# The last two pairs of a combined four-layer convolution: PSUM tiles, copies and output thirds rearranged

## The chip, the cores and the metric

The kernel runs on one core of a Trainium2 chip. The metric is the device time of one execution in microseconds (us), and the time of a kernel is the median of its runs. Engines are named as in the profile: PE is TensorE's matmul, PEld its weight load, DVE is VectorE, ACT is ScalarE, POOL is GpSimd, SP is SyncE, whose queue issues the transfers.

## What is computed

A batch of 128 samples, each with 64 channels of 1024 positions, goes through four convolutions of 3 taps. They are of the types same, upsample, same and downsample, with a blur of four taps beside each change of the rate. The weights of each layer are scaled by a style of the sample and normalised (demodulated), so each sample has its own weights. The input is added to the result.

```python
s = style @ mw.T + mb
weight = SCALE * w * s[:, None, :, None]
demod = lax.rsqrt(jnp.sum(weight * weight, axis=(2, 3)) + EPS)
weight = weight * demod[:, :, None, None]
...
for i, typ in enumerate(TYPES):
    out = _layer(out, style, weights[i], biases[i], mod_w[i], mod_b[i], typ)
return out
...
x = x + _L0_cond_ref(x, cond_512, L0_cond_weights, L0_cond_biases, L0_cond_mod_w, L0_cond_mod_b)
```

All data are float32.

## The kernel before, in words

**One convolution for four.** Between the ends of the signal, four linear layers are one convolution of 9 taps with a 64 x 64 matrix per tap and sample. The kernel builds these weights on TensorE for four samples at a time (a quad, index q, 32 of them): stage1, stage2 and stage3 multiply the weights of the layers into each other, and each stage's PSUM result is scaled and copied to SBUF by ACT (line 330). The result is `Wf`. combine (lines 452 to 463) makes three sums of it, h1, h2 and h3 in tile `H`, on DVE. The few positions near the ends are computed apart, spread over the rounds, and do not touch the change.

**Pairs of samples.** The convolution itself runs over pairs of samples (index p, 64 of them, two per quad). The positions of a sample lie in three planes (position modulo 3), and in two halves of 170 per plane. A fast scheme gives the three output planes with five products instead of nine:

- pre1 and pre2 (lines 480 to 526) form the five combinations of the input planes, tile `T`, on DVE and POOL;
- product (line 528) is one of the five products: 12 matmuls in each of two banks, one bank for each sample of the pair (a float32 matmul has two records in the profile, so 48 records are two products and 24 are one);
- convA12 computes products 1 and 2 and convA3 product 3 into the tile `psA`; convA3 also has ACT copy the first product, negated, to SBUF (`m1`, line 567);
- seed (seed1 and seed2, lines 572 to 599, all through line 573) combines the three on DVE: it makes `u` and `v`, writes the third output plane `y1` to SBUF, and writes a start value of the first two planes into a PSUM tile (`Y` in the profile). seed_last does the same in another order, the PSUM part first;
- convB adds products 0 and 4 onto the start values in PSUM;
- output (line 622) scales and shifts the planes into the tile `o`: planes 0 and 1 from PSUM in one instruction of 340 columns, the third from `y1` in one of 170 columns. On ACT that is line 630, on DVE line 632;
- store (line 634) issues the transfer of one sample to memory from SP's queue. It waits for the output of that sample, and later stores wait behind it.

[...] Fresh banks therefore get matmuls of zeros first (zeros_to_y, line 164, matmuls at line 170).

**PSUM.** There are eight banks of 512 columns. The pool `ps_conv` has two tiles of two banks each (`psA`, in turn for even and odd pairs), `ps_y` has the one tile `Y` of two banks, and `ps_w` has two tiles of one bank each, which the weight stages use. The helper unit gives two banks of a pool:

```python
if pool is ps_w:
    return [pool.tile([P, 512], F32, tag=f"u{r}", name=f"{name}_{r}") for r in range(2)]
t = pool.tile([P, 2, 512], F32, tag="u", name=name)
return [t[:, r, :] for r in range(2)]
```

So two banks from `ps_w` are two tiles, and two banks from `ps_conv` are one tile. All pairs use `Y` except those in the dictionary Y2, which y_bank (line 161) looks up. When the weight stages have ended, the banks of `ps_w` are free: before, pairs 60 and 62 have these, and pair 63 takes a `ps_conv` tile (Y3). Pair 61 uses `Y`.

**The order.** The order of the program is the order on each engine's queue (manual_schedule), and the framework adds the waits between the engines. A round q of the loop at line 1061 runs convB and the outputs of pairs 2q and 2q+1, convA12 and convA3 of the pairs after them, and the weight stages of later quads. In the last three rounds:

- round 29 (p = 58) makes the last weights; the zeros go to the banks of pair 60 (lines 1130 to 1134), then seed(60), combine(31), convA12(61) and convA3(61);
- round 30 (p = 60, the branch q == NQ - 2) runs convB(60), the outputs of 60, convA12(62), seed(61), pre2(63), convA3(62), convA12(63), convB(61), output(61, 0) by ACT, seed(62), convA3(63), the zeros of 63, output(61, 1) by DVE and seed_last(63);
- round 31 (p = 62, q == NQ - 1) runs convB(62), its outputs by ACT and DVE, convB(63), and the outputs of 63 plane by plane: third, first, second, sample 0 by ACT and sample 1 by DVE each time. The first two planes are stored apart, so 63 has four stores, two of 170 columns and two of 340.

Of the kernel before, what the change touches and what calls it, by code (L numbers as in the profile page):

```python
# [49 lines left out]
AF = mybir.ActivationFunctionType  # L50
# [13 lines left out]
def kernel(  # L64
# [13 lines left out]
    NQ = B // 4  # L78
# [5 lines left out]
    nc_v, nc_a, nc_g = nc.vector, nc.scalar, nc.gpsimd  # L84
# [13 lines left out]
    ps_conv = ctx.enter_context(tc.tile_pool(name="ps_conv", bufs=2, space=PSUM))  # L98
# [48 lines left out]
    def unit(pool, name):  # L147
# [7 lines that stand above are left out]
    NB = 170  # L155
# [3 lines left out]
    Y2 = {}  # L159

    def y_bank(p, s):
        return Y2[p][s] if p in Y2 else Y[:, s]

    def zeros_to_y(sets, n, p=0):


        for i in range(sets):
            rows = HALF[i % 2]
            for cols in HALF:
                nc.tensor.matmul(  # L170
                    y_bank(p, i % 2)[cols, :n], Z[rows, :C], Z[rows, :n], start=True, stop=True
                )
# [51 lines left out]
    def var_inverse(bs, ls=slice(0, NL)):  # L224
        nc_v.reciprocal(dm[:, ls, bs], nw[:, ls, bs])
# [241 lines left out]
    HO = 3 * NB  # L467
    Ts = {}
    Gs = {}
    part = {}  # L470
# [53 lines left out]
    def pre2(p):  # L524
        pre2a(p)
        pre2b(p)

    def product(p, m, ps):

        W, H_ = Wq[p // 2]  # L530
        r0 = p % 2
        for g in range(3):
            for s, rows in enumerate(HALF):
                for h, cols in enumerate(HALF):
                    if m in (0, 4):
                        w = W[rows, r0, K * g + m // 2, :]
                    else:
                        w = H_[rows, m - 1, r0, g, :]
                    j = NB * h + g
                    nc.tensor.matmul(  # L540
                        ps[s][cols],
                        w,
                        Ts[p][rows, SLOT[m], j : j + NB],
                        start=(g == 0 and m not in (0, 4)),
                        stop=(g == 2),
                        skip_group_check=True,
                    )

    def m_tile(tag, p, shape=(2, NB)):
        return mpool.tile([P, *shape], F32, tag=tag, name=f"{tag}_{p}")  # L550

    def convA12(p):
        if p >= NP:
            return
        ps = ps_conv.tile([P, 2, 512], F32, tag="u", name=f"psA{p}")
        m = [ps[:, :, i * NB : (i + 1) * NB] for i in range(3)]
        product(p, 1, [m[0][:, s] for s in range(2)])
        product(p, 2, [m[1][:, s] for s in range(2)])
        part[p] = m

    def convA3(p):
        if p >= NP:
            return
        m = part[p]
        product(p, 3, [m[2][:, s] for s in range(2)])
        m1 = m_tile("m1", p)
        nc_a.activation(m1, m[0], AF.Copy, scale=-1.0)  # L567
        part[p] = (m1, *m[1:])

    y1s = {}  # L570

    def sum_of(out, x, f, y):
        nc_v.scalar_tensor_tensor(out, x, f, y, op0=ALU.mult, op1=ALU.add)  # L573
# [12 lines left out]
    def seed2(p):  # L586
        if p >= NP:
            return
        m3, u = part.pop(p)
        banks = [(slice(s, s + 1), y_bank(p, s)[:, None]) for s in range(2)]  # L590
        if p not in Y2:
            banks = [(slice(0, 2), Y)]
        for i, f in enumerate((1.0 / 6.0, 4.0 / 6.0)):
            for k, y in banks:
                sum_of(y[..., i * NB : (i + 1) * NB], m3[:, k], f, u[:, k])

    def seed(p):
        seed1(p)
        seed2(p)

    def seed_last(p):

        m1, m2, m3 = part.pop(p)
        u, v = m_tile("u", p), m_tile("v", p)
        y1s[p] = mpool.tile([P, 2, NB], F32, tag="y1", name=f"y1_{p}", bufs=3)
        sum_of(u, m2, -1.0 / 3.0, m1)
        part[p] = m3, u
        seed2(p)
        sum_of(v, m2, 1.0 / 3.0, m1)
        sum_of(y1s[p], m3, 2.0 / 6.0, v)  # L610
# [11 lines left out]
    def output(p, s, eng=nc_a, parts=((0, 2), (2, 3))):  # L622

        b = 2 * p + s
        d3, add = dm[:, 3, b : b + 1], oc[:, b : b + 1]
        for i, j in parts:
            dst = os[p][:, s, i * NB : j * NB]
            src = y1s[p][:, s] if i == 2 else y_bank(p, s)[:, i * NB : j * NB]
            if eng is nc_a:
                nc_a.activation(dst, src, AF.Identity, bias=add, scale=d3)  # L630
            else:
                eng.tensor_scalar(dst, src, d3, add, op0=ALU.mult, op1=ALU.add)

    def store(p, s, at=slice(0, 3 * NB)):
        nc.sync.dma_start(out[p, :, s, at], os[p][:, s, at])
# [100 lines left out]
    def zeros():  # L736
        for t in Ye:
            nc_g.memset(t[:, :, 0:1], 0.0)
            nc_g.memset(t[:, :, 7:8], 0.0)
        for t in Ue:  # L740
            nc_g.memset(t[:, :, 0:1], 0.0)
            nc_g.memset(t[:, :, 10:11], 0.0)
        for t in Ve:
            nc_g.memset(t[:, :, 0:2], 0.0)
            nc_g.memset(t[:, :, 10:12], 0.0)
        nc_g.memset(g1, 0.0)
# [142 lines left out]
    BOTH = nc_a, nc_v  # L889
# [171 lines left out]
    for q in range(NQ):  # L1061
        p = 2 * q
        c, s = q + 2, q + 3
        if q == 1:
            nc.sync.dma_start(Xe, x_ends)
        if q == 5:
            zeros()
        if c < NQ:
            stage2(c)
        convB(p)  # L1070
        output(p, 0)

        if c < NQ:
            stage3(c, 0)
        output(p, 1, nc_a if q < NQ - 1 else nc_v)
        if q == NQ - 1:
            store(p, 0)
            store(p, 1)

            convB(p + 1)  # L1080
            for i in (2, 0, 1):
                for r, eng in enumerate(BOTH):
                    output(p + 1, r, eng, ((i, i + 1),))
                    if i != 2:
                        store(p + 1, r, slice(0, NB) if i == 0 else slice(NB, HO))
            break
        convA12(p + 2)
        if q:
            if q < 3:

                (seed2 if q == 1 else seed)(p + 1)
            if q < NQ - 2:
                pre2(p + 3)
            store(p, 0)
            pre1(p + 4)
            store(p, 1)
            if q > 2:
                seed(p + 1)
            if q == NQ - 2:
                pre2(p + 3)  # L1100
        else:
            store(p, 0)
            store(p, 1)
            seed2(p + 1)
            var_inverse(PART[1])
            var_newton(PART[1])
            table_A(PART[1], dm[:, 2, PART[1]])
            for of in (table_C, vector_c0, table_3, vector_Da):
                of(PART[1])
            pre2(p + 3)  # L1110
            pre1(p + 4)
        EXTRA.get((q, 0), lambda: None)()
        if c < NQ:
            stage3(c, 1)
        convA3(p + 2)
        if q == NQ - 2:
            convA12(p + 3)
        side = SLOTS.get(q)
        convB(p + 1, (lambda: slot(*side)) if side else None)
        output(p + 1, 0)  # L1120
        if q == NQ - 2:
            seed(p + 2)
            convA3(p + 3)

            Y2[p + 3] = unit(ps_conv, "Y3")
            zeros_to_y(2, 2 * NB, p + 3)
        output(p + 1, 1, nc_a if q < NQ - 2 else nc_v)
        if q == NQ - 2:
            seed_last(p + 3)
        if c == NQ - 1:  # L1130

            banks = unit(ps_w, "Y2")
            Y2[p + 2] = Y2[p + 4] = banks
            zeros_to_y(2, 2 * NB, p + 2)
        if q:
            pre2(p + 4)
            store(p + 1, 0)
            pre1(p + 5)
            store(p + 1, 1)
        if q < NQ - 2:  # L1140
            seed(p + 2)
        if s < NQ:
            stage1(s)
        if s + 1 < NQ:
            scale3(s + 1)
        if c < NQ:
                combine(c)
        if q == 0:
            store(p + 1, 0)
            store(p + 1, 1)  # L1150
            pre2(p + 4)
        EXTRA.get((q, 1), lambda: None)()
        if q < NQ - 2:
            convA12(p + 3)
            convA3(p + 3)
        if q == 0:
            seed1(p + 3)
            pre1(p + 5)
# [66 lines left out]
```

## Time and profile before

| what | value |
|---|---|
| median of 3 runs | 500.7 us (499.32 to 501.7) |
| profiled execution, its own time | 501.05 us |
| its span, first to last instruction | 499.2 us |
| mean granted TensorE clock | 0.993 |
| DVE, busy share of the span | 89% |
| ACT | 65% |
| POOL | 27% |
| stores `out<-o`, 255 KB, median from issue to landing | 2.8 us |
| stores `out<-o`, 170 KB | 2.5 us |
| stores `out<-o`, 85 KB | 2.2 us |

The times come from one profiled execution and are counted from the start of its span. A row of the timeline has the start, the length, the engine, the line, the operation, the tiles as out<-in with the shape, the count of merged instructions, and in brackets the idle time of the engine before it with what ended it. Instructions of DVE and ACT overlap a little in the records: one begins before the one before it has left the pipeline, unless it waits for it. The chain of waits names the work that ended last, followed back from the end.

### The profile page before, as it was taken

The numbers are of one execution on the slowest core, as the hardware profiler recorded it, in microseconds if no ns is written. First come the engines' busy times: TensorE is split into PE (matmuls) and PEld (weight loads), VectorE is DVE, ScalarE is ACT, GpSimd is POOL, SyncE is SP. The second block draws the span as 40 slices with busy tenths as digits, with TensorE's granted clock in tenths as the row PEclk, the third lists the DMA queues.
The fourth block names the chain that finished last, engine by engine and source line by source line (L and its number), as shares of the span: only waits on it lengthen the run. The fifth ranks groups of instructions, "written<-read, shape, count | busy, mean of one in ns | idle before, by whom it ended". The sixth has DMA issues, their size and how long they took to land.

```text
span 499.2 us, 28320 instructions
## 1 busy us (share of the span) xinstructions
PE 487.2 (98%) x12616; PEld 474.9 (95%) x12616; DVE 444.0 (89%) x937; ACT 322.5 (65%) x788; POOL 133.7 (27%) x195
## 2 busy tenths in 40 slices
PE   7999999899999999999999999999999999999994
PEld 5899989899999999999999999999999999999994
DVE  4989999999999979987979998879999889888895
ACT  4546757567666667667667667657667666766643
POOL 2234315345222212212222122212212212221210
PEclk8999999999999999999999999999999999999998
DMA  8125535454444445353445444435355435443123
GB/s 260 46 61 170 178 116 169 144 171 140 147 146 149 145 137 164 126 164 122 144 145 161 127 157 153 144 124 163 125 146 165 141 123 189 148 141 130 69 106 127
DMA packets 37449, 70.90 MB, mean 142 GB/s; under 512 B 4176, under 2 KB 28752, under 8 KB 37328
## 3 DMA queue, kind: packets, MB, share of 16 engines
q1 hardware_dynamic: 37248, 68.85, 43.0%
q8 instruction: 99, 1.62, 1.4%
q10 hardware_dynamic: 80, 0.25, 0.1%
q14 instruction: 22, 0.18, 0.1%
HBM read 35.46 MB, written 33.62 MB: 138 GB/s over the span
## 4 chain that ended last, share of the span: by engine, by line
PE 85%; DVE 11%; issue 1%; ACT 1%; DMA 1%; SPq 0%; DVEq 0%
PE psA L540 29%; PE Y L540 19%; PE psR L383 15%; PE psW L420 13%; PE psS L352 6%; PE psE L780 2%; DVE T L522 2%; DVE G L489 2%; DVE Y L573 2%; DMA par_oi<-in_params_oi 1%; DVE G L494 1%; DVE u L573 1%; DVE T L512 1%; DVE v L573 1%; DVE H L458 0%
## 5 line engine op out<-in xcount | busy, mean ns | idle before, releaser
L540 PE MATMUL psA<-T,H 64*64 64x170 f32 x4608 | 207.9, 304 | 0.5 <-ACT R L330 0.3
L540 PEld LDWEIGHTS psA<-T,H 64*64 64x64 f32 x4608 | 190.8, 133 | 1.4 <-issue 0.8
L540 PE MATMUL Y<-T,Wf 64*64 64x170 f32 x3072 | 141.9, 304 | 3.1 <-DVE Y L573 2.8
L500 POOL TENSOR_TENSOR T<-G 128x342 f32<-128x342 f32 x62 | 57.6, 929 | 318.5 <-DVE G L494 189.7
L540 PEld LDWEIGHTS Y<-T,Wf 64*64 64x64 f32 x3072 | 128.8, 133 | 5.7 <-issue 2.3
L630 ACT ACTIVATE o<-Y,oc,dm 128x340 f32<-128x340 f32 (+1 forms) x126 | 79.8, 634 | 60.1 <-PE Y L540 59.4
L420 PE MATMUL psW<-R,par_oi 64*64 64x256 f32 (+3 forms) x1536 | 100.2, 349 | 0.0
L573 DVE SCALAR_TENSOR_TENSOR Y<-psA,u 128x340 f32<-128x340 f32 (+1 forms) x134 | 66.7, 502 | 35.2 <-ACT o L630 32.9
L383 PE MATMUL psR<-S,E 64*64 64x192 f32 (+1 forms) x2304 | 93.9, 299 | 0.4 <-ACT S L330 0.4
L330 ACT ACTIVATE Wf<-psW,t 128x256 f32<-128x256 f32 (+1 forms) x252 | 75.3, 381 | 23.3 <-PE psW L420 23.1
L420 PEld LDWEIGHTS psW<-R,par_oi 64*64 64x64 f32 x1536 | 86.2, 133 | 3.1
L383 PEld LDWEIGHTS psR<-S,E 64*64 64x64 f32 x2304 | 86.9, 133 | 0.6 <-ACT S L330 0.5
L330 ACT ACTIVATE R<-psR,tC 128x448 f32<-128x448 f32 x63 | 36.5, 630 | 56.0 <-PE psR L383 56.0
L630 ACT ACTIVATE o<-y,oc,dm 128x170 f32<-128x170 f32 x125 | 65.8, 526 | 0.4 <-DVE y L573 0.4
L501 POOL TENSOR_TENSOR T<-G 128x342 f32<-128x342 f32 x62 | 58.6, 946 | 0.0
L522 DVE TENSOR_TENSOR T<-G 128x684 f32<-128x684 f32 x64 | 57.0, 890 | 0.0
L489 DVE SCALAR_TENSOR_TENSOR G<-X 128x688 f32<-128x688 f32 x64 | 56.9, 889 | 0.0
L352 PE MATMUL psS<-wd,par_oi 64*64 64x192 f32 x768 | 46.1, 329 | 0.0
L352 PEld LDWEIGHTS psS<-wd,par_oi 64*64 64x64 f32 x768 | 38.4, 136 | 0.5 <-ACT raw L648 0.3
L567 ACT ACTIVATE m<-psA 128x340 f32<-128x340 f32 x64 | 29.2, 456 | 10.1 <-PE psA L540 4.9
L573 DVE SCALAR_TENSOR_TENSOR y<-psA,v 128x340 f32<-128x340 f32 x64 | 32.7, 511 | 2.2
L494 DVE SCALAR_TENSOR_TENSOR G<-X 128x342 f32<-128x342 f32 x64 | 33.2, 519 | 0.0
(132 smaller groups left out, 384.7 us busy)
## 6 DMA issues: line engine op xcount, KB each, us to landing
out<-o SPq DMA_DIRECT2D x126, 255.0 KB, 2.8
X<-in_x SPq DMA_DIRECT2D x60, 344.0 KB, 3.1
X<-in_x SPq DMA_DIRECT2D x60, 172.0 KB, 3.2
X<-in_x SPq DMA_DIRECT2D x4, 516.0 KB, 6.5
Xe<-in_x_ends SPq DMA_DIRECT2D x1, 512.0 KB, 3.6
par_oi<-in_params_oi SPq DMA_DIRECT2D x2, 208.0 KB, 4.8
out<-o SPq DMA_DIRECT2D x2, 170.0 KB, 2.5
par_io<-in_params_io ACTq DMA_DIRECT2D x1, 240.0 KB, 3.8
```

The costliest lines, as they stand in the source:

```text
L330: nc_a.activation(dst, src, AF.Copy, scale=f)
L352: nc.tensor.matmul(ps[r][cols, k * C : (k + K) * C], woi[rows, 2, k, :], src[rows, :], start=(k == 0), stop=(k == K - 1), skip_group_check ...
L383: nc.tensor.matmul(ps[r][cols, lo * C : (lo + m) * C], E[rows, e + 2, :], src[rows, a, :], start=(n == 0), stop=(n == 8), skip_group_check ...
L420: nc.tensor.matmul(ps[r][cols, (lo - t_lo) * C : (hi - t_lo) * C], woi[rows, 0, k, :], rt[c][rows, lo - k : hi - k, :], start=(k == order[0]),
L489: nc_v.scalar_tensor_tensor(g[:, PL:], X[:, : 2 * PL], 0.5, X[:, PL:], op0=ALU.mult, op1=ALU.subtract)
L494: nc_v.scalar_tensor_tensor(plane(g, 2), plane(X, 3), 0.5, plane(X, 2), op0=ALU.mult, op1=ALU.subtract)
L500: eng.tensor_add(t[:, 2, :NJ], plane(g, 2), plane(g, 1))
L501: eng.tensor_sub(t[:, 3, :NJ], plane(g, 2), plane(g, 1))
L522: nc_v.tensor_sub(t[:, 0:2, :NJ], both(a, PL), both(b, 1))
L540: nc.tensor.matmul(ps[s][cols], w, Ts[p][rows, SLOT[m], j : j + NB], start=(g == 0 and m not in (0, 4)), stop=(g == 2), skip_group_check=True,
L573: nc_v.scalar_tensor_tensor(out, x, f, y, op0=ALU.mult, op1=ALU.add)
L630: nc_a.activation(dst, src, AF.Identity, bias=add, scale=d3)
```

## The change

In the last rounds, pairs 61 and 63 now have the two bank tiles of `ps_w`, and 60 and 62 use `Y`. The zeros of round 29 go to the banks of 61, and the zeros of 63 and its tile Y3 are gone. ACT's copy of the first product is a function of its own; for 63 it stands right behind convA12(63). output(61, 1) stands between convA3(63) and seed_last(63) as before, but its third plane goes to GpSimd, and so do the third planes of sample 1 of pairs 62 and 63. For 63, the third planes come first and are stored apart, and the first two planes follow in one instruction of 340 columns per sample.

```diff
--- before.py
+++ after.py
@@ -558,14 +558,16 @@
         product(p, 2, [m[1][:, s] for s in range(2)])
         part[p] = m
 
-    def convA3(p):
+    def copy_m1(p):
+        m1 = m_tile("m1", p)
+        nc_a.activation(m1, part[p][0], AF.Copy, scale=-1.0)
+        part[p][0] = m1
+
+    def convA3(p, copy=copy_m1):
         if p >= NP:
             return
-        m = part[p]
-        product(p, 3, [m[2][:, s] for s in range(2)])
-        m1 = m_tile("m1", p)
-        nc_a.activation(m1, m[0], AF.Copy, scale=-1.0)
-        part[p] = (m1, *m[1:])
+        product(p, 3, [part[p][2][:, s] for s in range(2)])
+        copy(p)
 
     y1s = {}
 
@@ -1072,17 +1074,19 @@
 
         if c < NQ:
             stage3(c, 0)
-        output(p, 1, nc_a if q < NQ - 1 else nc_v)
-        if q == NQ - 1:
+        if q < NQ - 1:
+            output(p, 1)
+        else:
+            output(p, 1, nc_v, ((0, 2),))
+            output(p, 1, nc_g, ((2, 3),))
             store(p, 0)
             store(p, 1)
 
             convB(p + 1)
-            for i in (2, 0, 1):
-                for r, eng in enumerate(BOTH):
-                    output(p + 1, r, eng, ((i, i + 1),))
-                    if i != 2:
-                        store(p + 1, r, slice(0, NB) if i == 0 else slice(NB, HO))
+            for i, j, engs in ((2, 3, (nc_a, nc_g)), (0, 2, BOTH)):
+                for r, eng in enumerate(engs):
+                    output(p + 1, r, eng, ((i, j),))
+                    store(p + 1, r, slice(i * NB, j * NB))
             break
         convA12(p + 2)
         if q:
@@ -1115,23 +1119,23 @@
         convA3(p + 2)
         if q == NQ - 2:
             convA12(p + 3)
+            copy_m1(p + 3)
         side = SLOTS.get(q)
         convB(p + 1, (lambda: slot(*side)) if side else None)
         output(p + 1, 0)
         if q == NQ - 2:
             seed(p + 2)
-            convA3(p + 3)
-
-            Y2[p + 3] = unit(ps_conv, "Y3")
+            convA3(p + 3, lambda p: None)
+            output(p + 1, 1, nc_v, ((0, 2),))
+            output(p + 1, 1, nc_g, ((2, 3),))
+            seed_last(p + 3)
+        else:
+            output(p + 1, 1)
+        if c == NQ - 1:
+
+            banks = unit(ps_w, "Y2")
+            Y2[p + 3] = Y2[p + 5] = banks
             zeros_to_y(2, 2 * NB, p + 3)
-        output(p + 1, 1, nc_a if q < NQ - 2 else nc_v)
-        if q == NQ - 2:
-            seed_last(p + 3)
-        if c == NQ - 1:
-
-            banks = unit(ps_w, "Y2")
-            Y2[p + 2] = Y2[p + 4] = banks
-            zeros_to_y(2, 2 * NB, p + 2)
         if q:
             pre2(p + 4)
             store(p + 1, 0)
```

More of the change, by code (lines that the diff above doesn't have):

```diff
@@ L1122 @@
             seed(p + 2)
-            convA3(p + 3)
-            Y2[p + 3] = unit(ps_conv, "Y3")
-            zeros_to_y(2, 2 * NB, p + 3)
-        output(p + 1, 1, nc_a if q < NQ - 2 else nc_v)
-        if q == NQ - 2:
+            convA3(p + 3, lambda p: None)
+            output(p + 1, 1, nc_v, ((0, 2),))
+            output(p + 1, 1, nc_g, ((2, 3),))
             seed_last(p + 3)
+        else:
+            output(p + 1, 1)
         if c == NQ - 1:
             banks = unit(ps_w, "Y2")
-            Y2[p + 2] = Y2[p + 4] = banks
-            zeros_to_y(2, 2 * NB, p + 2)
+            Y2[p + 3] = Y2[p + 5] = banks
+            zeros_to_y(2, 2 * NB, p + 3)
         if q:
```

## The prediction

> **What bounds the kernel now.** I read four views in this order: the busy table, the chain of waits for the last 16 us, the timelines of DVE and ACT for the stretch the diff touches, and GpSimd's groups of instructions.
>
> ```profile
> PE 487.2 (98%) x12616; PEld 474.9 (95%) x12616; DVE 444.0 (89%) x937; ACT 322.5 (65%) x788; POOL 133.7 (27%) x195
> ```
>
> TensorE is busy from end to end, and all but the last three of 32 rounds are untouched by the diff. So only the tail, 476 us on, can change, and there the chain of waits is read (start, length, what):
>
> ```profile
> 482.99 3.09 PE psA L540 x72
> 486.08 1.76 PE Y L540 x48
> 487.84 0.02 issue
> 487.87 0.64 ACT o L630
> 488.51 0.03 issue
> 488.54 0.91 DVE o L632 x2
> 489.44 0.43 DVE u L573
> ...
> 491.10 0.35 DVE Y L573
> 491.45 0.04 issue
> 491.50 2.00 PE Y L540 x48
> 493.50 0.02 issue
> 493.53 0.50 ACT o L630
> 494.03 0.03 issue
> 494.05 0.46 DVE o L632
> 494.52 0.02 issue
> 494.54 0.50 ACT o L630
> 495.04 0.03 issue
> 495.07 0.46 DVE o L632
> ```
>
> Two parts of the end are not TensorE's. From 487.84 to 491.50 the outputs of pair 61 (ACT, then DVE) and then the seed of 63 hold back 63's last products, while TensorE has other work until 490.76 and idles 0.52. From 493.50 to 495.53 four outputs of 63 run strictly one after another, ACT, DVE, ACT, DVE. The span ends at 499.2, 3.67 after the last of them (the last store is issued at 495.55 and lands at 498.20).
>
> **Why they take turns.** ACT reads sample 0, DVE sample 1: two banks, but one PSUM tile (Y for 61, Y3 for 63). The Trainium skill, PSUM — Partial Sum Buffer, section "PSUM bank collisions raise a hardware error", asks to guard by bank and quadrant only; by that rule these could run together and separate bank tiles would gain nothing at the end. The trace differs: DVE starts at 488.54, just when ACT's 340-wide read of Y is over, although ACT is still writing the same o tile until 488.92. So the whole two-bank tile is guarded, not o. Where each bank has its own tile, both do run together (ACT, then DVE, at the first round):
>
> ```profile
> 11.54 0.53 ACT L330 ACTIVATE S<-psS,tB 128x320 f32<-128x320 f32 x1 [1.17 <-PE psS L352]
> 11.62 0.55 DVE L332 TENSOR_SCALAR S<-psS,tB 128x320 f32<-128x320 f32 x1 [2.34 <-PE psS L352]
> ```
>
> I go by the row.
>
> **Part 1, pairs 60 and 61 swap tiles (a loss).** Before, the seed of 60 went to fresh banks, without a wait; now it goes to Y and must wait until ACT has read 59 out of it.
>
> ```profile
> 477.27 0.51 DVE L573 SCALAR_TENSOR_TENSOR y<-psA,v 128x340 f32<-128x340 f32 x1
> 477.70 1.06 DVE L573 SCALAR_TENSOR_TENSOR Y<-psA,u 128x170 f32<-128x170 f32 x4
> 478.67 0.55 DVE L458 SCALAR_TENSOR_TENSOR H<-Wf 128x384 f32<-128x384 f32 x1
> ```
>
> ACT's last 340-wide read of 59 starts at 477.67 and takes 0.62: 478.29. With 0.02 of signalling the seed starts at 478.31 instead of 477.70, so 0.61 later. The seed itself costs the same in either tile (2 instructions of 340 take DVE 0.97 until the next, 4 of 170 into separate tiles also 0.97). Behind it in DVE's queue stand the six steps of combine(31) and the seed of 61, with no idle time until 483.97. TensorE waits for this seed: the products of 63 in convA12 reuse the psA buffer of 61. Its weight loads show an idle 0.23 until 484.08, and the first product comes 0.15 after DVE's end. So no slack is left and TensorE is 0.61 later from there: convB(61) starts at 486.48, not 485.87. Convolutions in between have the cover: convB(60) starts 0.27 later (479.52, behind the seed), h1 of combine is ready at 481.16, about when convB(60) is through (481.25). The eight zero matmuls of round 29 stay; they only clear 61's banks instead of 60's.
>
> **Part 2, the copy of 63's first product sooner.** It moves from behind convA3(63) to before convB(61) in ACT's queue. It adds one wait: convA3(63) writes the bank that the copy reads. The copy (0.44 to 0.45) can run as soon as convA12(63) is done, 486.8 to 487.25; TensorE comes to convA3(63) at 488.21. The 1.73 of convB(61) hides it. Without that cover it would cost 0.45.
>
> **Part 3, 61's outputs and the seed of 63.** Round 30, all 0.61 later: convB(61) is signalled at 488.45. ACT (sample 0) and DVE (sample 1) now start together at 488.48; DVE is free for the next at 489.03, as the 0.36 third goes to GpSimd. What is late next is not this but convA3(63): u reads m2 from a bank that convA3 still writes, and the trace holds such reads (the copy of 62 waits until convA3(62) is through, 0.92). Its signal was at 488.71, now 489.32. Then u 0.50 and 0.03: the first Y at 489.88. The four Y into Y3 cost 0.377 each, because each waits for the one before in one tile; into separate tiles 0.241 each (477.70 to 478.67). So the last ends at 489.88 + 3 x 0.241 + 0.34 = 490.94, and convB(63) starts at 491.00 instead of 491.50. The eight zero matmuls that go (488.46 to 489.03 on TensorE, 0.57) are not on this path: convB(62) would now be through at 490.80, so TensorE idles 0.2 before 63. Net of parts 1 to 3: -0.50.
>
> **Part 4, the outputs of 63.** Products end at 493.00. ACT and DVE each take one instruction of 340 (0.634 and 0.632) side by side: 493.66. SP issues one store of 170 KB at 493.68 and the other after it; issues follow each other by 0.40 (0.33 each and a semaphore). So the last issue is 1.07 after the products' end, before it was 2.05: -0.98. Stores of 63 stay four of the same sizes, the two small ones now first: with 62's two before them they leave at about 492.1, 492.5, 492.9 and 493.3, just clear of 493.68. Landing and closing 3.65, as before.
>
> **Part 5, thirds by GpSimd.** No row shows this form. From below: a TENSOR_SCALAR of 64x48 took 0.37; from above: a two-input TENSOR_TENSOR of 128x342 took 0.93, with twice the width and inputs. I take 0.6; range 0.37 to 0.93. For 63, y is ready at about 491.93, so GpSimd is through by 492.9 even at the dear end, and SP wants it at 493.3: cost zero.
> The rule that speaks against it: SBUF — State Buffer, section "Who interferes with whom", says that a DVE instruction with two SBUF inputs and a GpSimd one that reads SBUF exclude each other. The trace agrees in an early stretch, where T<-G usually takes 0.86:
>
> ```profile
> 56.17 1.59 DVE L522 TENSOR_TENSOR T<-G 128x684 f32<-128x684 f32 x1
> ```
>
> Beside it GpSimd's sum took 1.20 instead of 0.92. In the tail the third of 61 runs from about 483.7 to 484.3; DVE's two-input pre2(63) starts at 484.48. Should they meet, DVE loses up to 0.7, against 0.34 of idle time before output(61,1) and 0.3 before u: at most 0.1 is left. By the rule alone +0.7, by the row and its cover 0. The thirds of 62 and 63 meet only PSUM readers (Y, v, output).
>
> **Sum.** -0.50 - 0.98 = -1.48 us in a span of 499.2, thus 497.7, and 499.6 for the profiled execution (501.05, of which 1.85 lie outside the span). That execution is 0.35 above the median of 500.7. Off the median: 499.2; with a tenth for the second store's landing beside the first, **499.3 us**, -0.3%.
>
> **Rivals.**
> - A: the wait of 60's seed does not reach TensorE (for: TensorE has convA work queued; against: DVE shows no idle time and TensorE already idles there). Then convA3(63) is signalled at 488.71, the seed ends at 490.33, convB(63) starts at 490.39, -1.11, and with the end -2.1: 498.6.
> - B: the bank tiles are still guarded together, or o is. Then the Y cost 0.41 more, and DVE's last output follows ACT's (store at +1.34 rather than +1.07): -1.48 + 0.41 + 0.27 = -0.8: 499.9. Against it stands the row at 11.54.
> - C, the other side: GpSimd's third is slow in this form. It stands in SP's queue ahead of the two last stores, each 0.40, so with y at 491.93 it decides when it takes over 1.7 (493.68), and the kernel is slower than before from 2.8 (last issue at 495.55). At 3.5, say, +0.7: 501.4. The nearest row, 0.93, speaks against.
> - D: the change does nothing that is seen, since single runs of before spread by 2.4: 500.7.
>
> **Chances.** My forecast 0.60, A 0.14, B 0.13, C 0.05, D 0.08. Half a per cent, about what a measurement of this kernel can tell from no change, is 2.5 us; forecast, B and D lie inside it, A near its edge. Faster by over 0.5% 0.16, within 0.78, slower 0.06. The range takes in A with a spread of runs below it and D above: 497.7 to 500.9.
>
> **What would show it.** In the profile after: DVE's first Y of 60 at 478.3 with ACT as releaser; convA12(63) about 484.7; no zeros near 488.5; four overlapping Y near 490 and convB(63) at 491.0; ACT's and DVE's last outputs starting together near 493.0; GpSimd's thirds below 1 us. It is wrong if the third or the seed of 60 takes longer, or if the last outputs still alternate.

## The result, and the profile after

| what | before | after |
|---|---|---|
| first comparison, median | 501.73 us (12 runs) | 500.89 us (12 runs), ratio 0.999, interval 0.9975 to 1.0006 |
| second comparison, median | 501.19 us (44 runs) | 500.01 us (22 runs), ratio 0.9973, interval 0.996 to 0.9987 |
| profiled execution, its own time | 501.05 us | 498.96 us |
| its span | 499.2 us | 497.2 us |

The forecast was a ratio of 0.9972 (499.3 against 500.7). The two comparisons, 0.999 and 0.9973, differ by 0.0017, more than half the width of either interval, so the times alone do not settle whether the gain is 0.5 or 1.4 us. That the second one stands so near the forecast is luck, as the profiles will show: they give less, if they are read at the right place. The two spans differ by 2.0 us, but more than half of that is not the change. The first lines of two tables of windows, the kernel before first (window, its length, busy time and count for PE, PEld, DVE, ACT and POOL, then the granted clock, the DMA share and GB/s):

```profile
0.00:50.00 50.00, 47.09 (x1080) 41.54 (x1084) 39.77 (x105) 26.44 (x68) 17.02 (x48) 0.97 0.42 134
```

```profile
0.00:50.00 50.00, 47.91 (x1107) 42.03 (x1111) 41.08 (x107) 27.28 (x69) 17.29 (x48) 1.00 0.44 134
```

In the first 50 us, where both kernels do the same, the clock was 0.97 in one profile and 1.00 in the other, and the second has got further (1107 matmul records against 1080). The clock is not all of it: in the run with fewer bytes, below, it was 1.00 there too, and only 1054 records were done. What else moves this stretch stays open. DVE's last wide G (line 489, 688 columns), the last landmark ahead of the changed part, starts at 475.11 before and at 473.97 after: 1.14 us apart (in the run with fewer bytes it starts at 476.48). All that follows is therefore counted from the start of that instruction, and its distance to the end of the span is called the tail. The tail is 24.13 before and 23.21 after.

So the gain is 0.92 here. The tail in numbers, in us from that landmark, with what the forecast says when counted likewise (475.11 taken off its times):

| step | before | forecast | after |
|---|---|---|---|
| first Y of 60 | 2.59 | 3.20 | 3.21 |
| convA12(63), first matmul | 9.01 | 9.62 | 9.64 |
| u of 63 | 14.26 | 14.24 | 14.33 |
| convB(63), first matmul | 16.39 | 15.89 | 15.92 |
| products of 63 end | 18.39 | 17.89 | 18.04 |
| last output ends | 20.42 | 18.55 | 18.70 |
| last store is issued | 20.45 | 18.97 | 19.51 |
| end of the span (the tail) | 24.13 | 22.65 | 23.21 |

The forecast holds to 0.15 up to the last output and misses by 0.54 at the last store. From the chain of waits after (start, length, what), the start of convA12(63) at 483.61 and the end of the products of 63 at 492.01:

```profile
483.61 1.96 PE psA L540 x48
...
488.17 3.84 PE Y L540 x86
492.01 0.03 issue
492.04 0.63 DVE o L634
```

The rows of the profile after, in the order of the prediction's list. DVE, the seed of 60:

```profile
476.14 0.51 DVE L575 SCALAR_TENSOR_TENSOR y<-psA,v 128x340 f32<-128x340 f32 x1
477.18 1.08 DVE L575 SCALAR_TENSOR_TENSOR Y<-psA,u 128x340 f32<-128x340 f32 x2 [0.53 <-ACT o L632]
478.16 0.55 DVE L458 SCALAR_TENSOR_TENSOR H<-Wf 128x384 f32<-128x384 f32 x1
```

DVE now idles 0.53 in front of it, and ACT's output releases it. DVE, from the outputs of 61 to the end:

```profile
487.39 0.63 DVE L634 TENSOR_SCALAR o<-Y,dm,oc 128x340 f32<-128x340 f32 x1 [0.36 <-PE Y L540]
488.30 0.51 DVE L575 SCALAR_TENSOR_TENSOR u<-psA,m 128x340 f32<-128x340 f32 x1 [0.28 <-PE psA L540]
488.92 1.07 DVE L575 SCALAR_TENSOR_TENSOR Y<-psA,u 128x170 f32<-128x170 f32 x4
...
492.04 0.63 DVE L634 TENSOR_SCALAR o<-Y,dm,oc 128x340 f32<-128x340 f32 x1 [0.55 <-PE Y L540]
```

ACT's last output in the same profile, and GpSimd's thirds:

```profile
491.88 0.64 ACT L632 ACTIVATE o<-Y,oc,dm 128x340 f32<-128x340 f32 x1 [0.37 <-PE Y L540]
```

```profile
482.66 0.49 POOL L634 TENSOR_SCALAR o<-y,dm,oc 128x170 f32<-128x170 f32 x1 [5.20 <-ACT o L632]
486.21 0.49 POOL L634 TENSOR_SCALAR o<-y,dm,oc 128x170 f32<-128x170 f32 x1 [3.06 <-ACT m L563]
491.10 0.49 POOL L634 TENSOR_SCALAR o<-y,dm,oc 128x170 f32<-128x170 f32 x1 [4.40 <-ACT o L632]
```

Both engines wait for TensorE alone now, where before DVE waited for ACT and ACT for DVE. u waits for convA3 (psA), as forecast. The four Y take 1.07, and before, where each waits for the one ahead of it, 1.48:

```profile
489.36 0.50 DVE L573 SCALAR_TENSOR_TENSOR u<-psA,m 128x340 f32<-128x340 f32 x1
489.97 1.48 DVE L573 SCALAR_TENSOR_TENSOR Y<-psA,u 128x170 f32<-128x170 f32 x4
```

TensorE's weight loads for convB(63), after:

```profile
489.86 1.24 PEld L540 LDWEIGHTS Y<-T,Wf 64*64 64x64 f32 x34 [0.27 <-issue]
```

They start at 489.86, before the last Y has ended at 489.99. What is new stands in SP's queue. The last four issues before and the last four after (length in ns, minimum, median and maximum, then the starts):

```profile
L635 SPq DMA_DIRECT2D out<-o x4: 332/332/342, 494.0 to 495.6; - x4
```

```profile
L637 SPq DMA_DIRECT2D out<-o x4: 402/409/413, 492.0 to 493.5; - x4
```

The issues after, one by one from 491.5 on; the first is of pair 62, the next two are of the thirds of 63, and the last two are of its first two planes:

```profile
491.55 0.33 SPq L637 DMA_DIRECT2D out<-o  x1
```

```profile
491.97 0.41 SPq L637 DMA_DIRECT2D out<-o  x1
```

```profile
492.47 0.41 SPq L637 DMA_DIRECT2D out<-o  x1
```

```profile
492.98 0.41 SPq L637 DMA_DIRECT2D out<-o  x1
```

```profile
493.48 0.40 SPq L637 DMA_DIRECT2D out<-o  x1
```

The outputs had ended at 492.67, but the last store leaves at 493.48: the stores stand in a line, the last four 0.50 apart. And the DMA engines have become busy almost without a break. The same stretch of the tail (17.9 until the last data) in windows, before and then after; the share and the GB/s at the end of each row count:

```profile
493.00:494.00 1.00, 0.46 (x16) 0.15 (x5) 0.49 (x2) 0.47 (x1) 0.00 (x0) 1.00 0.60 235
494.00:495.00 1.00, 0.00 (x0) 0.00 (x0) 0.45 (x1) 0.48 (x2) 0.00 (x0) 1.00 0.75 285
495.00:496.00 1.00, 0.00 (x0) 0.00 (x0) 0.46 (x1) 0.03 (x1) 0.00 (x0) 0.95 0.57 179
496.00:497.09 1.09, 0.00 (x0) 0.00 (x0) 0.00 (x0) 0.00 (x0) 0.00 (x0) 0.50 0.89 293
```

```profile
491.87:492.87 1.00, 0.12 (x2) 0.00 (x0) 0.63 (x1) 0.64 (x1) 0.00 (x0) 1.00 0.98 369
492.87:493.87 1.00, 0.00 (x0) 0.00 (x0) 0.00 (x0) 0.00 (x0) 0.00 (x0) 1.00 0.95 316
493.87:495.01 1.14, 0.00 (x0) 0.00 (x0) 0.00 (x0) 0.00 (x0) 0.00 (x0) 1.00 0.90 315
```

Before, the data of the stores of 62 and 63 (1020 KB) took 4.2 us with pauses; after, 3.1 us at 0.90 to 0.98. The first data of 62 start at nearly the same place of the tail in both (17.81 before, 17.90 after), since its store is issued at 16.97 before and 17.07 after. So the change has squeezed out the pauses, and little more is left to squeeze.

### The profile page after: what moved, and what is told of

It reads as the page before. It is cut to its first block, busy times and chain, and to the rows that moved or that the text cites. A ratio compares the mean times of both kernels' runs of the same rounds, so it can differ in the third digit from the quotient of the medians.

```text
span 497.2 us, 28312 instructions
## 1 busy us (share of the span) xinstructions
PE 486.5 (98%) x12608; PEld 474.7 (95%) x12608; DVE 443.0 (89%) x931; ACT 322.6 (65%) x787; POOL 135.9 (27%) x198
## 4 chain that ended last, share of the span: by engine, by line
PE 88%; DVE 8%; ACT 1%; issue 1%; DMA 1%; DVEq 0%; ACTq 0%
PE psA L540 29%; PE Y L540 21%; PE psR L383 15%; PE psW L420 14%; PE psS L352 6%; PE psE L782 2%; DVE T L522 1%; DVE Y L575 1%; DVE G L489 1%; DMA par_s<-in_params_s 1%; PE Y L170 1%; DVE G L494 1%; DVE T L512 1%; PE Y L306 0%; DVE H L460 0%
## 5 line engine op out<-in xcount | busy, mean ns | idle before, releaser
L632 ACT ACTIVATE o<-Y,oc,dm 128x340 f32<-128x340 f32 x125 | 79.6, 637 | 57.8 <-PE Y L540 57.7
L352 PE MATMUL psS<-wd,par_oi 64*64 64x192 f32 x768 | 45.1, 323 | 0.0
L575 DVE SCALAR_TENSOR_TENSOR u<-psA,m 128x340 f32<-128x340 f32 x64 | 32.4, 506 | 1.2 <-ACT m L563 0.9
```

What stands on the lines that cost most here:

```text
L352: nc.tensor.matmul(ps[r][cols, k * C : (k + K) * C], woi[rows, 2, k, :], src[rows, :], start=(k == 0), stop=(k == K - 1), skip_group_check ...
```

## The experiments

Three theories of the missing half microsecond were set against each other: S, the issue on SP's queue; L, the DMA engines' time for the bytes; W, waits on DVE and TensorE that the forecast had missed. What is compared is the tail, in one profile of each kernel where nothing else is said.

**The kernels once more.** The changed kernel, twice, and the one before, once.

> The changed kernel once more, unchanged, to see how far one profile of the tail can be trusted. The tail is counted from the start of DVE's last wide G (line 489) to the end of the span: 24.13 us before, 23.21 after, so the change has brought 0.92 and not the forecast 1.48. Both theories (SP's queue; the seed's wait) expect 23.2 within 0.1 here, and the last output ending 18.7 and the last store issued 19.5 after that start.

> The changed kernel timed beside the others on one chip: tail 23.1 to 23.2, so 0.9 to 1.1 us below before, ratio 0.998.

> The kernel before once more, unchanged: the tail was 24.13 in its one profile, and three profiles of the changed kernel gave 23.21, 23.07 and 23.01. It should be 23.9 to 24.2, with the last output ending at 20.42 and the last issue at 20.45; then the gain in the profile is 0.8 to 1.1.

Measured: tails of 23.07 and 23.01 after, 24.20 before; the last output ends at 18.71, 18.69 and 20.43, the last issue is at 19.52, 19.50 and 20.45. So everything up to the last issue repeats within 0.02; the landing of the last store varies by 0.2. With three profiles after (mean 23.10) and two before (24.17) the gain is 1.07 us, 0.21% of 500.7, inside both intervals of the ratio. The timed run gave 0.9973, where 0.998 was expected and the profiles give 0.9979.

**Fewer stores.** The diff against the changed kernel:

```diff
                     output(p + 1, r, eng, ((i, j),))
-                    store(p + 1, r, slice(i * NB, j * NB))
+                    if i == 0:
+                        store(p + 1, r)
```

> The changed kernel, but pair 63 is stored in two stores of all three planes, as the other pairs are, instead of four. Theory S (SP's queue is the new end): the last output ends at 18.70 but the last store is issued at 19.51, since the six last stores leave one after another, 0.50 apart, each issue taking 0.41; with two stores fewer the last one is issued at 18.95 to 19.05 and the tail falls by about 0.5, to 22.7. Theory L (what counts is the landing of the bytes, not the issue): the same bytes, the third planes even later, so the tail stays at 23.2 or grows by 0.1 to 0.2. Theory W (the missing half microsecond lies in DVE's and TensorE's waits): no change, 23.2.

Measured: the last issue at 19.00, the tail 22.74, 0.36 below the mean of the changed kernel. That speaks against W only weakly, since the last data ended at 20.93 against 21.04 to 21.38, and most of the gain lies in the landing after it. What limits W is the table above: the last output ends within 0.15 of the forecast, and most of the miss stands behind it. This run does not separate S from L either, as I had thought it would.

**Two queues.**

```diff
-    def store(p, s, at=slice(0, 3 * NB)):
-        nc.sync.dma_start(out[p, :, s, at], os[p][:, s, at])
+    def store(p, s, at=slice(0, 3 * NB), q=nc.sync):
+        q.dma_start(out[p, :, s, at], os[p][:, s, at])
...
-                    store(p + 1, r, slice(i * NB, j * NB))
+                    store(p + 1, r, slice(i * NB, j * NB), nc_a if (i, r) == (0, 0) else nc.sync)
```

> The changed kernel, but the store of the first two planes of pair 63, sample 0, is issued from ACT's queue, right behind the output that it stores. The same four stores and bytes. Theory S: ACT issues it at 18.6 and SP the last one at 19.0 instead of 19.51, so the tail falls by about 0.5, to 22.7. Theory L: the same bytes at the same rate, 23.2. Theory W: 23.2.

Measured: ACT issued at 18.59 and SP its last at 19.03, as S expected, and the tail was 23.23. The issues came 0.5 earlier and nothing ended earlier (last data 20.98). S alone falls; the same windows of the tail in this run:

```profile
493.33:494.33 1.00, 0.14 (x2) 0.00 (x0) 0.63 (x1) 0.63 (x1) 0.00 (x0) 1.00 0.97 365
494.33:495.33 1.00, 0.00 (x0) 0.00 (x0) 0.00 (x0) 0.00 (x0) 0.00 (x0) 1.00 0.94 320
495.33:496.42 1.09, 0.00 (x0) 0.00 (x0) 0.00 (x0) 0.00 (x0) 0.00 (x0) 1.00 0.88 330
```

The engines are as full as with the later issues.

**Fewer bytes on the engines.**

```diff
-            store(p, 0)
-            store(p, 1)
+            store(p, 0, slice(0, 1))
+            store(p, 1, slice(0, 1))
```

> The changed kernel, but the two stores of pair 62 carry one column of 510 each (the rest of pair 62 is not written out): the same instructions on SP's queue, 510 KB less for the DMA engines. Theory S (the issue on SP sets the end) expects the last store issued at 19.5 and landing at 22.2 after the start of the last wide G, and a tail of 23.2 as in the changed kernel. Theory L (the DMA engines, which are busy without a break from 18.0 to 21.0 there, set it) expects the last issue at 19.5 too, but a landing 2.2 after it, at 21.7, and a tail of about 22.7.

Measured: the last issue at 19.40, the last data at 20.92, landing at 21.89, tail 22.92. The windows of the same stretch:

```profile
494.38:495.38 1.00, 0.13 (x2) 0.00 (x0) 0.63 (x1) 0.63 (x1) 0.00 (x0) 1.00 0.10 7
495.38:496.38 1.00, 0.00 (x0) 0.00 (x0) 0.00 (x0) 0.00 (x0) 0.00 (x0) 1.00 0.61 191
496.38:497.41 1.03, 0.00 (x0) 0.00 (x0) 0.00 (x0) 0.00 (x0) 0.00 (x0) 0.76 0.87 316
```

With 510 KB less the engines are nearly idle for a microsecond, and still the data end only 0.12 earlier. So L alone falls too: now the issue is the limit. The two lie at nearly the same place.

**Both relieved.** The last two diffs together.

> The changed kernel with both limits of the end relieved at once: the store of the first two planes of 63, sample 0, is issued from ACT's queue, and the two stores of 62 carry one column of 510 each (the rest of 62 is not written out). Each alone brought next to nothing: the last data ended at 20.98 and 20.92 instead of 21.04. If the issue on SP and the DMA engines are two limits that lie at one place, both together bring the last data to 20.4 to 20.5 (the last issue at 18.9, 0.5 to the first data, 1 us of engine time for two stores) and the tail to 22.3 to 22.6. If neither is the limit, the last data stay at 20.9 to 21.0.

Measured: last data at 20.73, tail 22.78. That gains more than either alone (20.98 and 20.92), but less than expected, 20.4 to 20.5. Behind the two limits the rows suggest a third, which no run tests: the output of sample 0 ends at 18.57, its store is issued at 18.60, its data start at 19.64, and the last two stores then take 1.1 us.

**Only the stores of 62 earlier.**

```diff
-        output(p, 0)
+        if q < NQ - 1:
+            output(p, 0)
...
-            output(p, 1, nc_v, ((0, 2),))
-            output(p, 1, nc_g, ((2, 3),))
+            for r, eng in enumerate(BOTH):
+                output(p, r, nc_g, ((2, 3),))
+                output(p, r, eng, ((0, 2),))
+            thirds.pop()()
```

Here `thirds` holds v and y of 63, taken out of seed_last.

> The changed kernel with only the outputs of 62 in another order: both thirds by GpSimd, DVE's output of 62 ahead of v and y of 63. The store of 62, sample 0, is issued 0.4 earlier (16.65 instead of 17.07) and sample 1 0.5 earlier, so the DMA engines have 62 behind them earlier; y of 63 comes 0.6 later, so the thirds of 63 are stored 0.1 to 0.2 later and the last issue on SP stays at 19.5 to 19.6. If the engines were the only limit, the last data end at 20.6 and the tail is 22.7; if SP's issue is the other, the last data stay at 21.0 to 21.1 and the tail at 23.0 to 23.2.

Measured: a miss, the tail was 23.71. I had overlooked that 62 sits in the undivided Y. DVE's rows, with what it waited for:

```profile
491.75 0.63 DVE L639 TENSOR_SCALAR o<-Y,dm,oc 128x340 f32<-128x340 f32 x1 [0.65 <-ACT o L637]
492.30 0.50 DVE L575 SCALAR_TENSOR_TENSOR v<-psA,m 128x340 f32<-128x340 f32 x1
492.84 0.51 DVE L575 SCALAR_TENSOR_TENSOR y<-psA,v 128x340 f32<-128x340 f32 x1
```

DVE waits 0.65 for ACT's read of 62, so v and y come 1.3 later than in the changed kernel (17.23 for v against 15.92), the thirds of 63 with them, and these stand ahead of the last two stores in SP's queue: last issue 20.25. A new wait had taken the place of the one removed.

**The swap of tiles undone.**

```diff
-            Y2[p + 3] = Y2[p + 5] = banks
-            zeros_to_y(2, 2 * NB, p + 3)
+            Y2[p + 2] = Y2[p + 4] = banks
+            zeros_to_y(2, 2 * NB, p + 2)
```

> The changed kernel with its swap of tiles undone: 60 and 62 in the two bank tiles as before, 61 and 63 in the one tile Y, no zeros for 63. If the wait of 60's seed is worth 0.61 on TensorE, as forecast: the seed of 60 has no wait behind ACT and the products of 63 in convA12 start 0.61 earlier, 9.03 instead of 9.64 after the start of the last wide G. DVE's outputs of 61 and of 63 wait for ACT's again, 0.6 each, since they share Y; so convB(63) starts only 0.2 to 0.35 earlier, the last output ends 0.3 later than in the changed kernel, and with SP's queue as the end the tail is 22.9 to 23.2. If the wait does not reach TensorE, convA12 of 63 stays at 9.64 and the tail grows by 0.3 or more.

> The run with 60 and 62 in the bank tiles and 63 in Y once more, now timed: its tail was 22.60 against 23.07 and 23.21 of the changed kernel. Ratio to before about 0.997, with the last output again at 19.07 and the tail 22.6 to 22.7.

Measured: convA12(63) at 9.02 instead of 9.64, the last output at 19.07, tails of 22.60 and 22.41, ratio 0.9966 (0.9953 to 0.9978). The seed of 60 runs without a wait:

```profile
477.11 0.51 DVE L575 SCALAR_TENSOR_TENSOR y<-psA,v 128x340 f32<-128x340 f32 x1
477.54 1.06 DVE L575 SCALAR_TENSOR_TENSOR Y<-psA,u 128x170 f32<-128x170 f32 x4
```

So the 0.61 of part 1 is real and reaches TensorE in full. (The chain after puts the wait of convA12(63) down to ACT's copy of 62. Here TensorE starts at 483.96 while that copy starts at 484.11, so it is the seed.) And though its last output ends 0.37 later, this kernel ends 0.6 earlier than the changed one in the profile: the store of 62, sample 0, is issued at 16.42 and the data of the last stores end at 20.6. So in the profiles the swap of tiles was a loss on the whole. The ratio of 0.9966 against 0.9973 cannot tell the two apart.

**Y divided.** As the last, with Y made of two tiles:

```diff
-    Y = ps_y.tile([P, 2, 512], F32, name="Y")
+    Y = [ps_y.tile([P, 512], F32, name=f"Y_{r}") for r in range(2)]
...
-        if p not in Y2:
-            banks = [(slice(0, 2), Y)]
```

> As the run with 60 and 62 in the bank tiles, but Y, too, is made of two tiles of one bank each. If reads wait for each other because two banks are one tile, ACT's and DVE's last outputs of 61 and 63 now start together, the last output ends about 0.9 earlier than with the undivided Y, at 18.1 to 18.2 after the start of the last wide G, and products of 63 still start at 9.0. If something else makes them take turns (the tile o), the last output stays at 19.1. For the tail, theory S (issue) expects 22.5 to 22.6, since store(62, 1), behind DVE's output of 62, comes earlier by what DVE gains; theory L the same within 0.1 of the run with the undivided Y, since the DMA engines have as much to carry after it.

Measured: last output at 18.12 instead of 19.07, tail 22.55. ACT's and DVE's last outputs, the undivided Y first and the divided Y second:

```profile
492.71 0.63 ACT L632 ACTIVATE o<-Y,oc,dm 128x340 f32<-128x340 f32 x1 [0.65 <-PE Y L540]
493.38 0.63 DVE L634 TENSOR_SCALAR o<-Y,dm,oc 128x340 f32<-128x340 f32 x1 [1.34 <-ACT o L632]
```

```profile
494.59 0.63 ACT L630 ACTIVATE o<-Y,oc,dm 128x340 f32<-128x340 f32 x1 [0.37 <-PE Y L540]
494.75 0.63 DVE L632 TENSOR_SCALAR o<-Y,dm,oc 128x340 f32<-128x340 f32 x1 [0.55 <-PE Y L540]
```

The division of Y was all that differed, so it is the common tile that made them take turns. But the tail stayed between those of the undivided Y (22.60 and 22.41), and the last data ended only about 0.14 earlier (20.46 against 20.6): 0.95 us of outputs were worth next to nothing at the end, since the engines carry the same bytes from nearly the same start (the store of 62, sample 0, is issued at 16.45 against 16.41).

**The late copy, and the thirds on DVE.**

```diff
             convA12(p + 3)
-            copy_m1(p + 3)
...
-            convA3(p + 3, lambda p: None)
+            convA3(p + 3)
```

> The changed kernel with the copy of the first product of 63 behind convA3(63), as before. By the forecast the copy, 0.45, then stands between convA3(63) and the seed: u of 63 starts 0.45 to 0.5 later (14.8 instead of 14.33 after the start of the last wide G), convB(63) 0.45 later and the last output ends at 19.15. Theory L: the stores of 62 and 63 come later by the same, the tail is 23.5 to 23.7. If the copy was never in the way, all stays at 14.33, 18.70 and 23.2.

Measured: u at 14.81, the last output at 19.11, tail 23.34. The early copy is worth 0.41 at the output and 0.36 at the last issue (19.87); at the end it is about 0.24, hardly more than the landing varies.

```diff
-            output(p, 1, nc_g, ((2, 3),))
+            output(p, 1, nc_v, ((2, 3),))
...
-            output(p + 1, 1, nc_g, ((2, 3),))
+            output(p + 1, 1, nc_v, ((2, 3),))
...
-            for i, j, engs in ((2, 3, (nc_a, nc_g)), (0, 2, BOTH)):
+            for i, j, engs in ((2, 3, (nc_a, nc_v)), (0, 2, BOTH)):
```

> The changed kernel with the three thirds on DVE instead of GpSimd. By the forecast the third of 61 (0.28 until the next instruction) fits into DVE's wait for convA3(63), so the seed of 63 stays where it is; the thirds of 62 and 63 fit before the last products end. The last output ends at 18.70 to 18.80 and the tail is 23.2 to 23.4. If GpSimd is what brings the gain, the last output ends 0.3 or more later.

Measured: u at 14.33 as with GpSimd, the last output at 18.70, tail 23.27. GpSimd brings nothing at the output; the last issue is 0.23 later (19.74), the tail 0.17 above the mean, which is no more than the landing varies.

**Two versions that use what was found.** Both with 60 and 62 in the banks, Y divided, v and y of 63 behind DVE's output of 62, and sample 0 of 63 stored from ACT's queue. The first keeps the four stores and gives both thirds of 62 to GpSimd, the second stores 63 in two.

> Y as two tiles, 60 and 62 in the bank tiles, and the stores of 62 as early as they can be: both thirds of 62 by GpSimd, DVE's output of 62 ahead of v and y of 63; the store of the first two planes of 63, sample 0, from ACT's queue. Theory L (the DMA engines carry the last 1.02 MB, some 3.0 us, without a break from the first data of 62 on): store(62, 0) is issued at 16.0 instead of 17.07 after the start of the last wide G, its data start at 17.0 instead of 18.0, the last data end at 20.0 to 20.3 instead of 21.0, and the tail is 21.9 to 22.3, against 24.1 before and 23.2 in the changed kernel: 2.0 us or 0.4% below before. If the end were set by the outputs alone (last output at 18.1 to 18.3, as in the run with a divided Y at 18.12), the tail would stay at 22.5.

> Y as two tiles, 60 and 62 in the bank tiles, DVE's output of 62 ahead of v and y of 63, and pair 63 stored in two stores of all three planes, sample 0 from ACT's queue and sample 1 from SP's. Theory L: the 510 KB of 63 can only start once its last output is there (18.1 and 1.0 to the first data) and take 1.35, so the last data end at 20.4 to 20.5 and the tail is 22.1 to 22.4. Theory S (issues): no queue is full, the last issue is at 18.15, and the tail is 18.15 + 2.2 + 1.0 = 21.4.

Measured: the first, tail 22.44, last data at 20.32 and last issue at 18.53; ratio 0.9956 (0.9939 to 0.9974). The second, tail 22.76, last data at 20.53; ratio 0.9941 (0.9922 to 0.996), from 6 runs. The data ended where L expected within 0.1, the tails were 0.1 to 0.4 longer than that, because the last store landed 1.1 and 1.2 after its last data. Both are faster than the kernel before, their intervals lie below 1. Against the changed kernel (0.996 to 0.9987) the interval of the first overlaps and that of the second only touches. The second has the lowest median (498.3 us), but the intervals of the two overlap widely, so which of them is faster is not shown. Nor is the size of their gain explained: their tails are 0.3 to 0.7 below the changed kernel's mean, their medians 1.3 and 1.7 below its median, and what the divided Y does in the earlier rounds is not examined here.

## Why the prediction was right and where it was wrong

The sum was forecast as -0.50 up to the end of the products of 63 and -0.98 from there to the last issue. In the first profiles it is -0.35, -0.59 and 0.02 for the landing: -0.92. The waits between the engines came as forecast. The step that failed is the second term, the one of the stores: it took issues in SP's queue to be 0.40 apart and the stores ahead to be clear of the last two, where the last four left 0.50 apart without a pause. It also put at nothing the time that the DMA engines need for the last megabyte.

- **Part 1 was right**, place and size: the seed of 60 at 3.21 (forecast 3.20), convA12(63) at 9.64 (9.62), and undoing the swap takes back 0.62.
- **Part 2 was right**: the copy is covered where it stands, and costs 0.41 to 0.48 where it stood.
- **Part 3 was right in its waits, and 0.15 too hopeful**: u waits for convA3(63), and the four Y overlap. But u started 0.09 later than forecast, and from its start to the first Y I took 0.53, where the rows before already had 0.61 (489.36 to 489.97) and those after have 0.62. So the last Y ended 0.18 later than forecast. That convB(63) still started 0.47 earlier than before (forecast 0.50) is luck: I had it wait for the last Y, but its weight loads began before the last Y had ended, since that Y was in the bank tile of sample 1 and the first matmuls write that of sample 0. (A product is twelve matmuls in all, six in each bank, 24 records, and not twelve in each as said further up.) The products then ended at 18.04 instead of 17.89. The zeros were not on the path.
- **Part 4 holds the error.** "Issues follow each other by 0.40", "just clear of 493.68": the 0.33 in it came from stores with pauses about them. In a full line the last four issues follow each other by 0.50, each taking 0.41. The store of (62, 1) also came 0.19 later than I had it, behind the late seed, v and y on DVE. With my 0.40 from there on, the last issue would stand at 19.18; so 0.21 of the miss of 0.54 is that late start, and 0.33 is the line. From the end of the products to the last issue I forecast 1.07; it is 1.47 (19.51 less 18.04), before 2.06. So the term -0.98 is -0.59 in the first profiles.
- **"Landing and closing 3.65, as before"** held, at 3.70 (3.55 and 3.51 in the repeats), but only because the issues were late. With two queues the last issue came at 19.03, close to the forecast 18.97, and yet the tail was 23.23: landing and closing took 4.20 there, while the DMA engines were 0.88 to 0.97 full. So issues without the line would not have brought the forecast end either. The sum -1.48 left out that the last megabyte needs 2.9 us of the engines' time from 17.9 on, whatever the outputs do.
- **Part 5 was right**: 0.49 (I took 0.6), and no contention in the tail: the third of 61 was over at 483.15 and T<-G of pre2(63) started at 483.79, and took 0.87 as it usually does. The two never met there, so the rule that the prediction set against this part was not put to the test in the tail.
- **The rivals.** A did not come: the wait reaches TensorE. B did not: the tile is what is guarded, as the divided Y shows. C did not: 0.49. The gain of 1.07 in the profiles lies between my forecast and D, by a cause that none of the four named. It is nearer to the -0.8 of B than to my -1.48, but that is chance, as what B says did not come. C had the right place, SP's queue, but the wrong reason for it.

What stays open: the time from the last data to the landing of the last store, 0.67 to 1.23 from run to run. It is as large as the differences in dispute here, and the runs show no cause. The size of the gain in time stays between 0.5 and 1.4 us by the two comparisons; 1.07 is what the profiles give.

## What to carry to other kernels

Where the end of a kernel is shortened, sum the stores as well as the outputs: count the bytes still to go at the rate of full DMA engines, from the first of the last stores on, and count the issues in their queue. In this kernel, outputs that ended earlier than that sum brought next to nothing, and an earlier first store was worth more than a faster last output. To judge a change in a tail of 24 us, measure from a landmark just ahead of it: here the landmark lay anywhere from 473.97 to 476.48 in kernels that do the same up to it.

## What the runs showed of the hardware that was not expected

A store issued right behind another takes longer on SP: 0.33 us alone, 0.37 to 0.41 directly behind another, and 0.50 from one to the next in the changed kernel (0.47 to 0.48 where the stores of 62 were of one column). The first data followed an issue by 0.83 to 0.89 us where the engines were free (0.83 for 62 in the changed kernel, 0.89 for the first third of 63 where the stores of 62 were of one column). In three profiles of the changed kernel, rows of 680 bytes took a DMA engine 35 to 36 ns on average, of 1360 bytes 59 to 60, of 2040 bytes 85 to 86: three planes in two stores cost 94 to 96 where one store costs 85 to 86, about a tenth more engine time. The last store landed 0.67 to 1.23 us after its last data, with no order in it that these runs show.
